# Order of the last stage of an attention and expert block: rotations two groups ahead across sequences, normalisation inside the next sequence

## The chip, the core and the metric

The kernel runs on one core of a Trainium2 chip. The metric is the device time of one execution in microseconds. Its engines are named as in the profile: PE is TensorE (matrix products; PEld its weight loads), DVE is VectorE, ACT is ScalarE, POOL is GpSimd, and SP issues most transfers.

## What is computed

The input x has 8 sequences of 512 tokens with 512 channels. A layer normalisation gives xn; an attention part s and a gate g are computed from it, and the output is x + s * g.

```python
xn = _layernorm(x, axis=-1)
s = _L0_attn_ref(xn, ...)        # linear attention, 16 heads of 32, chunks of 128 tokens
g = _silu(_L0_ffn_ref(xn, ...))  # 16 experts, the best 4 for each token, and a shared one
return x + s * g

# attention, for each sequence
q = _lrpe_rotate(silu(xn @ Wq)); k = _lrpe_rotate(silu(xn @ Wk)); v = xn @ Wv
scores = einsum('bthd,bshd->bhts', qi, ki) * D[None]
o_intra = einsum('bhts,bshd->bthd', scores, vi)
o_inter = einsum('bthd,bhde->bthe', qi * decay_q, S)
S_new = lam_C * S + einsum('bshd,bshe->bhde', ki * decay_k, vi)
x = o * sigmoid(xn @ Wg1 @ Wg2)
x = x * rsqrt(mean of squares over each head + EPS)   # the group normalisation
s = (x * weight) @ Wo
```

Everything is in float32.

## The kernel before

The kernel has three parts. The first normalises all sequences, routes their tokens, computes the shared expert and does the attention of sequences 0 and 1. The second runs the routed experts in blocks of 128 tokens. The third, the last stage, does the attention of sequences 2 to 7 and, beside it, gathers the experts' results for each token tile, adds them up and combines them with the attention's output. The change lies in the last stage.

A sequence's 16 heads are worked in four groups of four heads (G = 4, 128 channels each). For group g of sequence b:

- `key` and `query` (through `rotated`) multiply the transposed input xT by Wk or Wq (four matmuls of 128x512 output, L631), apply silu on ACT (L641), and rotate on DVE with a shuffle, a multiplication by cos, one by sin and an addition (L643 to L647). They write kT and qT, two buffers each.
- `by_token` transposes the rotated keys on PE (L663) and scales them on ACT into kd (L668). `scores` multiplies kd by the values for the states (L684), then keys by queries for all four heads (ps, L695); DVE adds up the states (L699), scales the queries (qd, L714) and multiplies each head's scores by the decay mask (sc, L720); ACT copies the states (L704).
- `output` multiplies states by queries and values by scores into po (L731, L742), and DVE multiplies po by the gate that is in `on` (L746).

`value` makes a tile of 128 tokens of values (pv, L587), copied out by ACT (L591). `gate_1` (L601) and `gate_2` (L617, sigmoid L621) make the gate. When all four groups have their outputs, `squares` (ACT L753, PE pr L756, square root on ACT L760), `inverse` (DVE L764) and `normed` (PE pb L773, four DVE multiplications L778) normalise; `project` multiplies a tile by Wo (pw, L785). The last sequence has forms of its own for its own normalisation (`squares_of`, `normed_of`, L884 to L908) and projection (L915).

PSUM has eight banks: four with tag "a" (the four ps of a group; also pr, pb and the gate), one "k" (transposes and states), one "m" (keys, and the even value tiles), two "d" (queries, odd value tiles, po, pw). Banks of a tag are used in turn, in the order in which the code asks for them, and a bank is free when its last reader is done.

The code of PE is written in its order by hand: `on_pe` ties each group of matmuls behind the one before. The other engines' queues are ordered by the framework's scheduler, except where `behind` ties an instruction to its engine's last one. Each engine works through its queue in order.

`step` in the last stage is `advance`. Each call carries the mixtures of a few token tiles a piece further: four gathers and two additions on POOL (L1215, L1221, L1224), two operations on DVE (m, L1226 and L1230), a silu on ACT (L1233). A new tile starts after every 2.2 calls. `finish` takes a projection's result: `last` multiplies it into the mixture on DVE (L1253; this is pw's reader) and adds x on POOL (L1257).

In `sequence` with `defer` set (sequences 2 to 6) the groups 0 and 1 hold keys and queries of groups 2 and 3 and two projections each of the sequence before; the groups 2 and 3 hold value tiles of the next sequence. After group 3, at the border, come the gate and the last value tile of the next sequence, `squares` and `inverse` of this one, then key, query of group 0, `normed`, key and query of group 1 of the next. `last_sequence` does sequence 7 and three of its groups project sequence 6.

Of the kernel before, what the change touches and what calls it, by code (L numbers as in the profile page):

```python
# [10 lines left out]
F32 = mybir.dt.float32  # L11
# [8 lines left out]
P = 128  # L20
# [3 lines left out]
C = 128  # L24
# [71 lines left out]
def tile_block(ctx: ExitStack, tc: tile.TileContext, a: dict, out: bass.AP):  # L96
# [553 lines left out]
    def key(b, g, ps=None):  # L650
        kT_of[g] = rotated(b, g, "k", wk, ps)

    def query(b, g):
        qT_of[g] = rotated(b, g, "q", wq)
# [94 lines left out]
    def squares(b):  # L749
        pr = bank("a", f"pr_{b}")  # L750
        for g in range(G):
            sq = scr[0].tile([P, N], F32, tag="sc", name=f"sq_{b}_{g}", bufs=4)
            nc.scalar.activation(sq, on_of[b][:, g, :], AF.Square)  # L753
            with on_pe():
                for c in range(NC):
                    nc.tensor.matmul(  # L756
                        pr[c * Q : (c + 1) * Q, :C], lhsT=sel[:, H - HG - g * HG :][:, :Q],
                        rhs=sq[:, c * C : (c + 1) * C], start=(g == 0), stop=(g == G - 1))
        rs = att.tile([P, C], F32, tag="tmp", name=f"rs_{b}", bufs=TMP)
        nc.scalar.activation(rs, pr[:, :C], AF.Sqrt, bias=eps_rms, scale=1.0)  # L760
        rs_of[b] = rs

    def inverse(b):
        nc.vector.reciprocal(rs_of[b], rs_of[b])  # L764
# [16 lines left out]
    def project(b, t):  # L781
        pw = bank("d", f"pw_{b}_{t}")
        with on_pe():
            for g in range(G):
                nc.tensor.matmul(  # L785
                    pw, lhsT=on_of[b][:, g, t * P : (t + 1) * P], rhs=wo[:, g, :],
                    start=(g == 0), stop=(g == G - 1))
        return pw
# [10 lines left out]
        query(b, 1)  # L799
        step()  # L800

    def sequence(b, step, projected, before=None, defer=False, also=lambda: None):


        n = b + 1

        def project_tiles(q, ts):
            if q is not None:
                for t in ts:
                    projected(q, t, project(q, t))  # L810


        fill = ([0], [1], [2], [3], [], [], [], [])
        for g in range(G):
            scores(b, g)
            step()
            if g + 2 < G:
                key(b, g + 2)
            else:
                value(n, 2 * (g - 2))  # L820
            if g + 1 < G:
                by_token(b, g + 1)
            project_tiles(before, fill[2 * g])
            step()
            if g + 2 < G:
                query(b, g + 2)
                if g + 3 == G and n not in xT_of:
                    load_xT(n)
            if g + 2 == G:
                value(n, 1)  # L830
            if g == 0 and b not in on_of:
                gate_2(b)
            project_tiles(before, fill[2 * g + 1])
            if fill[2 * g + 1] == [NC - 1]:
                on_of.pop(before, None)
            output(b, g)
            if defer and g + 2 == G:
                gate_1(n)
            step()
        v_of.pop(b)  # L840
        if n == FIRST:
            gate_1(n)
            squares(b)
            inverse(b)
            value(n, 3)
            normed(b)
            return
        if defer:
            gate_2(n)
        value(n, 3)  # L850
        also()
        squares(b)
        step()
        inverse(b)
        key(n, 0)
        also()
        query(n, 0)
        normed(b)
        also()
        if not defer:  # L860
            step()
        key(n, 1)
        by_token(n, 0)
        if defer:
            step()
        query(n, 1)
        also()
        if not defer:
            gate_1(n)
            project_tiles(b, [0, 1])  # L870
            also()
            project_tiles(b, [2, 3])
            also()
            on_of.pop(b)
        step()

    def last_sequence(b, step, projected, before):

# [43 lines left out]
        for g in range(G):  # L922
            scores(b, g)
            step()
            if g + 2 < G:
                key(b, g + 2)
            if g > 1:
                project_before(2 * g - 3)
            if g:
                squares_of(g - 1)  # L930
            if g + 1 < G:
                by_token(b, g + 1)
            step()
            if g + 2 < G:
                query(b, g + 2)
            if g in (1, 2):
                project_before(2 * g - 2)
                normed_of(g - 1)
            output(b, g)
            step()  # L940
# [357 lines left out]
        nc.gpsimd.memset(blocked[j], 0.0)  # L1298
    other.append(comb)
    enter(FIRST, ps=ahead[0])  # L1300
    for b in range(FIRST, B):
        if b + 1 < B:
            load_xT(b + 1)
            sequence(b, advance, finish, b - 1 if b > FIRST else None, True)
        else:
            last_sequence(b, advance, finish, b - 1)
    while active or late or steps[1] < len(tiles):
        advance()
    right.close()
# [54 lines left out]
```

## Time and profile before

| | us |
|---|---|
| median of 3 runs | 1167.91 (1167.41 to 1173.99) |
| the profiled execution | 1174.44 |
| its span | 1172.6 |
| first query product of the last stage starts | 724.56 |
| first key product of sequence 3, 4, 5, 6, 7 starts | 780.94, 854.93, 930.79, 1009.95, 1090.66 |
| ACT table loads in the last stage | 18 of 1.28 each |

The profile is of one execution. A line of the timeline gives the start, the time to the end of the merged instructions, the engine, the line of the code, the operation, the tiles written and read, and their sizes. Ends of matmuls are modelled, and the next one starts before the one before has ended; so durations of blocks on PE are taken from start to start. The four matmuls of a product are eight in the trace. A line of stretches gives, for each engine, busy time and number of instructions, then the granted clock of PE as a share, the share of the DMA engines and the rate.

### The profile page before, as it was taken

Reading aid. Unit: us, or ns where it says so; the run is one execution under the profiler, and the core shown is the slowest. Engines: PE = TensorE matmul, PEld = TensorE weight load, DVE = VectorE, ACT = ScalarE, POOL = GpSimd, SP = SyncE. Lnnn points to the kernel's source line nnn. Section 1 sums busy time; section 2 is a strip of 40 time slices with the busy share of each in tenths; the row PEclk is TensorE's granted clock in tenths of the full one; section 3 lists DMA queues with packets and bytes.
Section 4 is the critical chain, followed back from the end, with each engine's and each line's share of the span. In section 5 each row is a group of like instructions: output and inputs, shape, how many; then the busy total and the mean of one; then the engine's idle time right before and its main releaser. Section 6 shows DMA issues by size and latency. Waiting matters only on the chain. (4 is left out here: it accounts for less than half of the span.)

```text
span 1172.6 us, 21692 instructions
## 1 busy us (share of the span) xinstructions
PE 1138.4 (97%) x7780; PEld 697.9 (60%) x7780; DVE 713.8 (61%) x1496; ACT 460.9 (39%) x1042; POOL 451.9 (39%) x432
## 2 busy tenths in 40 slices
PE   7999999989999999999999999999999989999997
PEld 4455554456577776777777775555645545546453
DVE  6358726896134443444444445968979597697784
ACT  3224424255264443444444442253251522522541
POOL 3213103200223332333333332763877857858111
PEclk9999999998999999999999999999999999999999
DMA  9976421390769999889999996932747637534012
GB/s 333 316 268 216 157 97 46 111 350 1 230 151 228 231 227 219 226 229 228 220 237 225 234 225 207 337 100 93 259 117 220 189 105 245 147 122 145 19 38 72
DMA packets 163787, 217.45 MB, mean 185 GB/s; under 512 B 89824, under 2 KB 99168, under 8 KB 161760
## 3 DMA queue, kind: packets, MB, share of 16 engines
q1 hardware_dynamic: 142272, 144.14, 40.7%
q0 software_dynamic: 21120, 70.34, 22.1%
q8 instruction: 65, 1.06, 0.4%
q10 hardware_dynamic: 288, 1.57, 0.4%
q14 instruction: 42, 0.34, 0.1%
HBM read 125.73 MB, written 72.43 MB: 169 GB/s over the span
## 5 line engine op out<-in xcount | busy, mean ns | idle before, releaser
L1112 PE MATMUL pgu<-wexp,xt 128*128 x1088 | 257.6, 380 | 1.2 <-ACT xt L1093 0.7
L1112 PEld LDWEIGHTS pgu<-wexp,xt 128*128 128x128 f32 x1088 | 206.4, 190 | 87.5 <-issue 30.5
L1071 POOL DMA_INDIRECT xg<-xn_d,slot x79 | 74.9, 949 | 240.6 <-DVE y L1142 157.6
L1095 ACT COPY xt<-pl 128x512 uint16<-128x512 uint16 x136 | 104.3, 767 | 139.4 <-DMA pl<-xg 80.0
L1117 DVE TENSOR_TENSOR slb<-slb,pgu 128x128 f32<-128x128 f32 x136 | 39.1, 288 | 192.8 <-ACT slb L1116 192.8
L1215 POOL DMA_INDIRECT yg<-y_d,place x128 | 142.7, 1115 | 30.0 <-issue 18.2
L1133 PE MATMUL py<-wexp,hT 128*128 x272 | 139.3, 594 | 0.0
L587 PE MATMUL pv<-wv,xT 128*128 128x512 f32 x256 | 122.2, 614 | 3.8 <-DMA xT<-xT_d 2.7
L631 PE MATMUL pk<-xT,wk 128*128 128x512 f32 x256 | 118.3, 603 | 0.0
L631 PE MATMUL pq<-xT,wq 128*128 128x512 f32 x256 | 115.9, 593 | 0.3 <-PEq L1177 0.3
L785 PE MATMUL pw<-wo,on 128*128 128x512 f32 x224 | 105.7, 621 | 6.7 <-DVE m L1253 6.2
L1257 POOL TENSOR_TENSOR xo<-xo,m 128x512 f32<-128x512 f32 x31 | 45.6, 1471 | 136.3 <-DVE m L1253 128.2
L1071 POOL DMA_INDIRECT more<-xn_d,slot x57 | 53.8, 945 | 109.3 <-DVE y L1142 108.4
L720 DVE TENSOR_TENSOR sc<-ps,dmask 128x512 f32<-128x512 f32 x128 | 79.1, 677 | 1.0 <-PE ps L695 0.9
L631 PEld LDWEIGHTS pq<-xT,wq 128*128 128x128 f32 x256 | 47.3, 191 | 52.7 <-issue 51.7
L785 PEld LDWEIGHTS pw<-wo,on 128*128 128x128 f32 x224 | 43.0, 198 | 59.2 <-issue 48.7
L1142 DVE TENSOR_SCALAR y<-py,xg 128x512 f32<-128x512 f32 x79 | 59.3, 751 | 29.5 <-PE py L1133 29.3
L587 PEld LDWEIGHTS pv<-wv,xT 128*128 128x128 f32 x256 | 46.7, 195 | 50.2 <-issue 42.7
L631 PEld LDWEIGHTS pk<-xT,wk 128*128 128x128 f32 x256 | 46.2, 190 | 50.0 <-issue 47.5
L1116 ACT ACTIVATE slb<-pgu 128x128 f32<-128x128 f32 x136 | 37.9, 278 | 79.8 <-PE pgu L1112 79.3
L704 ACT COPY blocked<-state 32x96 f32<-32x96 f32 x96 | 30.7, 320 | 86.5 <-DVE state L699 85.6
L1142 DVE TENSOR_SCALAR y<-py,more 128x512 f32<-128x512 f32 x57 | 42.7, 750 | 19.7 <-PE py L1133 19.5
(173 smaller groups left out, 1738.4 us busy)
## 6 DMA issues: line engine op xcount, KB each, us to landing
y_d<-y SPq DMA_DIRECT2D x136, 256.0 KB, 3.1
wexp<-in_experts SPq DMA_DIRECT2D x14, 768.0 KB, 9.8
sh_d<-sh SPq DMA_DIRECT2D x32, 256.0 KB, 2.9
m<-sh_d SPq DMA_DIRECT2D x32, 256.0 KB, 4.7
xo<-in_x SPq DMA_DIRECT2D x32, 256.0 KB, 3.5
out<-xo SPq DMA_DIRECT2D x31, 256.0 KB, 2.2
x<-in_x SPq DMA_DIRECT2D x7, 1024.0 KB, 7.6
xT_d<-xT SPq DMA_DIRECT2D x7, 1024.0 KB, 8.5
```

What stands on the lines that cost most here:

```text
L587: nc.tensor.matmul(pv, lhsT=xT_of[b][:, k, t * P : (t + 1) * P], rhs=wv[:, k, :], start=(k == 0), stop=(k == KC - 1))
L631: nc.tensor.matmul(ps, lhsT=w[:, k, g * P : (g + 1) * P], rhs=xT_of[b][:, k, :], start=(k == 0), stop=(k == KC - 1))
L720: nc.vector.tensor_tensor(s, pss[j].rearrange("p (c t) -> p c t", t=C), dmask[:, g * HG + j].unsqueeze(1).to_broadcast([P, NC, C]), ALU.mult)
L785: nc.tensor.matmul(pw, lhsT=on_of[b][:, g, t * P : (t + 1) * P], rhs=wo[:, g, :], start=(g == 0), stop=(g == G - 1))
L1071: nc.gpsimd.indirect_dma_start(out=row(i), out_offset=None, in_=xn_d, in_offset=bass.IndirectOffsetOnAxis(ap=slot[:, i : i + 1], axis=0))
L1095: nc.scalar.copy(xt[:, KP:, :].bitcast(U16).rearrange("p k (t h) -> p h k t", h=2), turned(i).rearrange("p (h k) t -> p h k t", h=2))
L1112: nc.tensor.matmul(pg[:, : 2 * F], lhsT=xt[:, k, :], rhs=wflat[:, bass.ds(off + k * 2 * F, 2 * F)], start=(k == 0), stop=(k == KC - 1))
L1117: nc.vector.tensor_tensor(sl, sl, pg[:, F : 2 * F], ALU.mult)
L1133: nc.tensor.matmul(py, lhsT=hT_of.pop(i), rhs=wflat[:, bass.ds(off_of.pop(i) + KC * 2 * F, D)], start=True, stop=True)
L1142: gone.append(nc.vector.tensor_scalar(y, py, row(i).bitcast(F32)[:, bass.ds(at, 1)], None, ALU.mult).ins)
L1215: nc.gpsimd.indirect_dma_start(out=yg, out_offset=None, in_=y_d, in_offset=bass.IndirectOffsetOnAxis(ap=place[:, r, g : g + 1], axis=0))
L1257: nc.gpsimd.tensor_tensor(xo, xo, m, ALU.add)
```

## The change

Sequences 2 to 6 get a function of their own, `rolling`; `sequence` keeps only what sequences 0 and 1 use. In `rolling` each group has the key and the query that are two groups ahead, across the border into the next sequence; one value tile of the next sequence; and, from sequence 3 on, projections of the sequence before: one in group 1 ahead of the value tile and one after the query, one in group 2 and one in group 3. The first gate product is behind group 2's output, the second in group 3. `squares`, `inverse` and `normed` of the sequence before move from the border into group 0, also in `last_sequence`. The squares get their own tag with two buffers in the last stage, where they had four of the scores' tag, and rs gets its own buffer. The load of xT is issued after the query of group 1, one sequence further ahead, and once before the loop.

```diff
--- before.py
+++ after.py
@@ -749,14 +749,17 @@
     def squares(b):
         pr = bank("a", f"pr_{b}")
         for g in range(G):
-            sq = scr[0].tile([P, N], F32, tag="sc", name=f"sq_{b}_{g}", bufs=4)
+            sq = scr[0].tile(
+                [P, N], F32, tag="sq" if carry else "sc", name=f"sq_{b}_{g}",
+                bufs=2 if carry else 4)
             nc.scalar.activation(sq, on_of[b][:, g, :], AF.Square)
             with on_pe():
                 for c in range(NC):
                     nc.tensor.matmul(
                         pr[c * Q : (c + 1) * Q, :C], lhsT=sel[:, H - HG - g * HG :][:, :Q],
                         rhs=sq[:, c * C : (c + 1) * C], start=(g == 0), stop=(g == G - 1))
-        rs = att.tile([P, C], F32, tag="tmp", name=f"rs_{b}", bufs=TMP)
+        rs = scr[0].tile([P, C], F32, tag="rs", name=f"rs_{b}") if carry else att.tile(
+            [P, C], F32, tag="tmp", name=f"rs_{b}", bufs=TMP)
         nc.scalar.activation(rs, pr[:, :C], AF.Sqrt, bias=eps_rms, scale=1.0)
         rs_of[b] = rs
 
@@ -799,18 +802,10 @@
         query(b, 1)
         step()
 
-    def sequence(b, step, projected, before=None, defer=False, also=lambda: None):
+    def sequence(b, step, projected, also=lambda: None):
 
 
         n = b + 1
-
-        def project_tiles(q, ts):
-            if q is not None:
-                for t in ts:
-                    projected(q, t, project(q, t))
-
-
-        fill = ([0], [1], [2], [3], [], [], [], [])
         for g in range(G):
             scores(b, g)
             step()
@@ -820,7 +815,6 @@
                 value(n, 2 * (g - 2))
             if g + 1 < G:
                 by_token(b, g + 1)
-            project_tiles(before, fill[2 * g])
             step()
             if g + 2 < G:
                 query(b, g + 2)
@@ -828,14 +822,9 @@
                     load_xT(n)
             if g + 2 == G:
                 value(n, 1)
-            if g == 0 and b not in on_of:
+            if g == 0:
                 gate_2(b)
-            project_tiles(before, fill[2 * g + 1])
-            if fill[2 * g + 1] == [NC - 1]:
-                on_of.pop(before, None)
             output(b, g)
-            if defer and g + 2 == G:
-                gate_1(n)
             step()
         v_of.pop(b)
         if n == FIRST:
@@ -845,8 +834,6 @@
             value(n, 3)
             normed(b)
             return
-        if defer:
-            gate_2(n)
         value(n, 3)
         also()
         squares(b)
@@ -857,22 +844,57 @@
         query(n, 0)
         normed(b)
         also()
-        if not defer:
-            step()
+        step()
         key(n, 1)
         by_token(n, 0)
-        if defer:
-            step()
         query(n, 1)
         also()
-        if not defer:
-            gate_1(n)
-            project_tiles(b, [0, 1])
+        gate_1(n)
+        for ts in (range(NC // 2), range(NC // 2, NC)):
+            for t in ts:
+                projected(b, t, project(b, t))
             also()
-            project_tiles(b, [2, 3])
-            also()
-            on_of.pop(b)
+        on_of.pop(b)
         step()
+
+    def rolling(b, step, projected, before):
+
+
+        n = b + 1
+
+        def project_before(t):
+            if before is not None:
+                projected(before, t, project(before, t))
+
+        for g in range(G):
+            scores(b, g)
+            step()
+            ahead = (b, g + 2) if g + 2 < G else (n, g + 2 - G)
+            key(*ahead)
+            if g == 0 and before is not None:
+                squares(before)
+                inverse(before)
+            if g:
+                project_before((0, 2, 3)[g - 1])
+            if g + 1 == G:
+                on_of.pop(before, None)
+                gate_2(n)
+            step()
+            value(n, g)
+            by_token(*((b, g + 1) if g + 1 < G else (n, 0)))
+            query(*ahead)
+            if g == 1 and n + 1 < B:
+                load_xT(n + 1)
+            step()
+            if g == 0 and before is not None:
+                normed(before)
+            if g == 1:
+                project_before(1)
+            output(b, g)
+            if g + 2 == G:
+                gate_1(n)
+            step()
+        v_of.pop(b)
 
     def last_sequence(b, step, projected, before):
 
@@ -928,11 +950,16 @@
                 project_before(2 * g - 3)
             if g:
                 squares_of(g - 1)
+            else:
+                squares(before)
+                inverse(before)
             if g + 1 < G:
                 by_token(b, g + 1)
             step()
             if g + 2 < G:
                 query(b, g + 2)
+            if g == 0:
+                normed(before)
             if g in (1, 2):
                 project_before(2 * g - 2)
                 normed_of(g - 1)
@@ -1298,12 +1325,10 @@
         nc.gpsimd.memset(blocked[j], 0.0)
     other.append(comb)
     enter(FIRST, ps=ahead[0])
+    load_xT(FIRST + 1)
     for b in range(FIRST, B):
-        if b + 1 < B:
-            load_xT(b + 1)
-            sequence(b, advance, finish, b - 1 if b > FIRST else None, True)
-        else:
-            last_sequence(b, advance, finish, b - 1)
+        (rolling if b + 1 < B else last_sequence)(
+            b, advance, finish, b - 1 if b > FIRST else None)
     while active or late or steps[1] < len(tiles):
         advance()
     right.close()
```

## Prediction

> **What bounds the kernel now.** I read the page first, then the busy times of the last stage cut at the first key product of each sequence, then what TensorE waited for, then its instructions in order of time with those of ACT and DVE beside them.
>
> ```profile
> span 1172.6 us, 21692 instructions
> PE 1138.4 (97%) x7780; PEld 697.9 (60%) x7780; DVE 713.8 (61%) x1496; ACT 460.9 (39%) x1042; POOL 451.9 (39%) x432
> ```
>
> TensorE sets the time. What the change can win is the time in which TensorE waits in the last stage, and what it can lose is new waits there. Each stretch below holds one border of sequences and the groups up to the next (us, then busy us and count for each engine, the granted clock, DMA):
>
> ```profile
> 780.94:854.93 73.99, 73.99 (x645) 40.63 (x645) 59.70 (x92) 28.18 (x64) 42.78 (x35) 1.00 0.47 154
> 854.93:930.79 75.86, 74.56 (x645) 40.49 (x645) 63.13 (x93) 29.31 (x66) 58.33 (x50) 1.00 0.60 182
> 930.79:1009.95 79.16, 76.20 (x645) 41.37 (x645) 62.37 (x94) 28.72 (x65) 56.92 (x47) 0.98 0.53 165
> 1009.95:1090.66 80.71, 77.52 (x645) 41.96 (x645) 63.13 (x92) 28.05 (x64) 58.07 (x48) 0.98 0.45 135
> ```
>
> The same 645 matmuls take 73.99, 75.86, 79.16 and 80.71 us. DVE is busy for 60 to 63 us of them, so it has room on average, and is late only in places. TensorE in order of time, two pieces (a bracket gives the idle time before, and what ended it):
>
> ```profile
> 1016.94 1.18 PE L773 MATMUL pb<-rs,wge 16*128 16x128 f32 x32
> 1021.91 3.60 PE L631 MATMUL pq<-xT,wq 128*128 128x512 f32 x8
> 1025.44 0.40 PE L684 MATMUL pk<-v,kd 128*32 128x32 f32 x24
> 1025.84 2.95 PE L695 MATMUL ps<-qT,kT 32*128 32x128 f32 x32
> ```
> ```profile
> 961.81 5.40 PE L785 MATMUL pw<-wo,on 128*128 128x512 f32 x8 [2.96 <-DVE m L1253]
> 967.04 0.83 PE L731 MATMUL po<-qd,blocked 128*128 128x128 f32 x6
> 967.80 1.08 PE L742 MATMUL po<-sc,v 128*32 128x128 f32 x32
> 968.70 0.37 PE L684 MATMUL pk<-v,kd 128*32 128x32 f32 x24
> 969.00 1.17 PE L695 MATMUL ps<-qT,kT 32*128 32x128 f32 x32
> ```
> ```profile
> 1041.53 5.40 PE L785 MATMUL pw<-wo,on 128*128 128x512 f32 x8 [1.91 <-DVE m L1253]
> ```
>
> The two projections run at half the clock after their wait: 5.2 us from start to start where others take 3.43, so 1.8 us each. The scores at 1025.84 take 2.9 us instead of 1.1, because their four PSUM banks are freed by the four multiplications of `normed` (L778), here on DVE, with two lines of ACT:
>
> ```profile
> 1016.21 2.27 DVE L645 TENSOR_TENSOR kT<-sk,cos 128x512 f32<-128x512 f32 x1
> 1021.10 0.73 DVE L643 STREAM_SHUFFLE swq<-sq 128x512 f32<-128x512 f32 x1
> 1025.11 2.47 DVE L778 TENSOR_TENSOR on<-on,pb 128x512 f32<-128x512 f32 x4
> 1028.60 0.67 DVE L645 TENSOR_TENSOR kT<-sk,cos 128x512 f32<-128x512 f32 x1
> ```
> ```profile
> 1013.66 1.28 ACT L641 ACT_TABLE_LOAD   x1 [1.71 <-PE pk L631]
> ```
>
> **What it removes.** The excess over 73.99 is 1.9 + 5.2 + 6.7 = 13.8 us. The waits account for most: four times a projection behind DVE (6.2 us in the list of waits), two half-clock pieces (3.6), the scores (1.8), the group sums at 1088 (1.1). In the new order a group has key, [projection], value, transposes, query, [projection], output. A projection's PSUM bank is wanted again after a value product and transposes (3.8 us) instead of a query product (3.4), and a group has one projection, one group two, where two groups had two each. I credit all 13.8, 0.8 for a pause at 760.6 in sequence 2, and 1.6 because a sequence has 10 instead of 12 runs of wide products (a run's last product costs 3.63 instead of 3.43: 2 x 0.2 x 4 sequences). Sum: 16.2.
>
> **What it adds.** The number of matmuls and DMAs stays. New is where `squares` and `normed` of sequence b-1 stand: in group 0 of sequence b (3 to 7, five times), between the scores of group 0 and of group 1, which use the same four "a" banks. Three waits follow.
>
> *Scores of group 1 behind `normed`.* Let E be the end of group 0's query product. TensorE then has pb 1.10 (1016.94 to 1018.04), output 1.66 and state products 0.30 (967.04 to 969.00), and wants the scores at E + 3.06. Before, a key and a query product stood in between. In the built order DVE has the query rotation ahead of the multiplications: silu starts at E + 0.15 and takes 0.60, the shuffle starts at E + 0.79; shuffle 0.62, cos 0.60, sin 0.72, add 0.69 (start to start, undisturbed), four multiplications 2.47: E + 5.89. That is a wait of 2.8 us at least. POOL is busy for over half of these stretches, and an operation like the one at 1016.21 takes 2.27 instead of 0.67 beside it; by the means of their groups (cos 1.05, add 1.09 against 0.68) this adds 0.8. In sequences 4, 5 and 6 the order has one mixture operation (means 0.90 and 0.98, I take 0.9) ahead as well. In 3, 4 and 7 ACT's table load follows its wait for the query product, as at 1013.66, and adds 1.28. So 2.8 + 0.8 + 1.3 = 4.9, then 5.8, 4.5, 4.5 and, with POOL busy for 10 of the last 81 us, 2.8 + 1.3 = 4.1: 23.8. Without any collision it is 20.0 (a mixture operation then adds 0.65), with both operations hit as at 1016.21 in sequences 3 to 6 it is 33.
>
> *Group sums (`pr`) after group 0's key.* The squares get two buffers instead of four. Two wait for nothing; the third and fourth stand on ACT behind the key's silu: key end + 0.2 + 0.60 + 0.62 + 0.52 + 0.1 and the last part 0.25 make 2.3 us for a block of 1.0, so 1.3. The first part also needs the first score bank read. From the end of the query product before, TensorE is there after 1.66 + 0.30 + 1.10 + 3.54 = 6.6. In 4 and 5 DVE needs 0.79, rotation 2.63, the output's gate 0.60, three mixture operations 2.0, state 0.28, qd 0.47 and the first score 0.68: 7.4, by the means of the groups 1.7 more. That is 0.8 to 2.5 late, and the two squares then follow (0.25 + 0.2 + 0.62 + 0.52 + 0.1 + 0.25 - 1.0 = 0.9): 1.7 to 3.4. In 3 and 6 it has one mixture operation, no qd, but starts behind the output: 6.6, by the means 7.7, so 1.3 to 2.0. I take 2.0 + 3.4 + 3.4 + 2.0 + 1.3 = 12.1; low 7.3, high 15 if DVE is as late in all of 3 to 6.
>
> *Key and value in one bank.* Values 0 and 2 use bank "m", like the key. In sequence 2 nothing stands between: 0.2 + 0.60 + 0.1 of silu, twice, 1.8. Later a projection or the group sums hide it.
>
> *The clock.* Both waits of 1.9 and 3.0 us in the rows were followed by half clock, 1.8 us each; waits of 4 to 6 us should be too, but part of the slow stretch then falls into the wait. I take 1.3 x 5 = 6.5; 3.6 if two of five are hit, 9 if all in full.
>
> The Trainium skill ("TensorE: Matmul & The Clock Gate", "What's actually happening") speaks against a gap too, but has the clock fall after at least one idle window of about 3.4 us. These rows fell after less. By the page only a wait that covers a whole window costs, so perhaps two of the five: the sum would be some 4 us lower; I go by the rows.
>
> **Priced at nothing.** `load_xT` for two sequences on now waits on SP for group 1's query product; it lands in 8.5 us and is wanted some 45 us later; if SP were held up by outputs, its 8.5 us would show at value 0. Five more table loads (23 against 18, 1.28 each) fall on an ACT busy for 28 us of 75; the three on the path are counted. There are 16 instead of 15 `advance` calls a sequence; POOL's queue, with its gathers behind the additions L1257, waited 128 us for DVE and so runs ahead; if it did not, DVE's mixture operations and then the scores would wait, 1 to 3 us a tile. In groups 1 and 3 the query product waits for DVE's reading of the projection; value product and transposes give 3.8 us, and DVE reaches it about 1.8 us earlier; that margin gone, each us costs one.
>
> **Sum.** 23.8 + 12.1 + 1.8 + 6.5 - 16.2 = 28.0 us. The profiled execution took 1174.44 (span 1172.6 and 1.8 around it), so 1202. The median of the runs is 1167.91, 6.5 less, and I put the same difference on it: 1196. All low ends give 20.0 + 7.3 + 1.8 + 3.6 - 16.2 = +16.5, 1184; all high ends, with 13 won, 33 + 15 + 1.8 + 9 - 13 = +46, 1214.
>
> **Rivals.**
> A. *The border waits are hidden and the gain stays.* Break-even is (16.2 - 1.8) / 5 = 2.9 us a border. If DVE took the multiplications as soon as `pb` is there, they would end at E + 1.2 + 2.47, a wait of 0.6; with the squares ready in time and no fall of the clock: 1167.9 - 16.2 + 1.8 + 3 = 1156; with 1.3 a border for the squares 1163. For it: DVE has 11 us to spare in a sequence, and the first stretch shows next to no wait. Against: the built order has the rotation first, and one engine works in order. 12%, half of it over 1% faster.
> B. *The waits are there but shorter.* No collisions, no clock fall beyond one or two, half of the sums' wait: 20 + 3.6 + 1.8 + 2 - 16.2 = +11, 1179. For: an evener load gives DVE slack. Against: the means of the rows. 14%.
> C. *DVE never catches up after a border*: the query product of group 1 waits for L1253, by as much as it has in hand (1.8), and the clock falls twice a border (1.8): 5 x 3.6 = 18 more, 1214. For: 63 us of DVE work. Against: 17 us of TensorE work before group 1's output. 8%.
> D. *The change doesn't do what it says.* The built order has two rotations, one value product and about one projection in every group, so I give it nothing of its own.
>
> The forecast has 66%. About 1% (11.7 us) is what a measurement of this kernel can tell from no change. Faster by more: 0.06. Within: 0.06 of A and most of B, 0.15. Slower by more: 0.79. The range 1172 to 1211 leaves out A and C.
>
> **What would show it.** Right: TensorE's list of waits names L778 (scores) and ACT's squares (`pr`) once a border, the waits on L1253 are gone, sequences 3 to 6 last 80 to 84 us each, the clock falls near the borders. Wrong: stretches of 74 to 76 us, scores of group 1 with 1.2 us everywhere, or DVE multiplying right after `pb`.

## The result and the profile after

The changed kernel takes 1217.07 us (median of 4 runs, 1216.09 to 1217.75) against 1168.75 for the kernel before beside it: a ratio of 1.0389, 95% interval 1.0359 to 1.0419. It is 3.9% slower. The forecast, 1196 with a range of 1172 to 1211, had the direction and the places, but was 21 us too low. The profiled execution took 1217.75.

The head of the page after:

```profile
span 1216.0 us, 21663 instructions
PE 1159.6 (95%) x7780; PEld 710.7 (58%) x7780; DVE 695.6 (57%) x1496; ACT 468.8 (39%) x1047; POOL 447.1 (37%) x432
```

The span grew by 43.4 us and TensorE's busy time by 21.2 with the same 7780 matmuls. DVE has the same 1496 instructions and was busy for less, so nothing was added to it; it is needed at a worse moment. The last stage cut at the scores of group 0 of each sequence, so that each of these four stretches holds one sequence (3 to 6) with the normalisation of the one before (us, then busy us of each engine, granted clock, DMA):

```profile
800.28:883.60 83.32, 78.45 (x654) 43.48 (x644) 55.33 (x95) 30.20 (x65) 49.71 (x42) 0.96 0.47 149
883.60:969.01 85.41, 78.93 (x654) 44.00 (x644) 60.83 (x96) 30.21 (x65) 59.63 (x51) 0.96 0.54 169
969.01:1055.69 86.68, 80.55 (x655) 43.63 (x644) 63.48 (x95) 30.78 (x66) 58.91 (x50) 0.96 0.51 164
1055.69:1139.64 83.95, 79.22 (x654) 42.83 (x644) 52.12 (x90) 30.03 (x64) 36.22 (x31) 0.96 0.26 78
```

All four take 83 to 87 us (the prediction named 80 to 84), where the four of before took 74 to 81, and the granted clock is 0.96 in each instead of 0.98 to 1.00. What TensorE waited for in the last stage (total us, times, longest):

```profile
PE ps L695 <- DVE on L781: 14.8, 8, 3.0
PE pr L758 <- ACT sq L755: 5.2, 5, 1.5
PE pr L758 <- DVE sc L720: 3.8, 2, 2.5
PE pv L587 <- ACT sk L641: 3.8, 2, 3.0
```

The list names the waits that the prediction named: scores behind the multiplications of `normed` (now L781), the group sums behind ACT's squares and behind the first score bank, a value behind its key's silu. The projections' waits for their reader (6.2 us before) are gone. One border in order of time, sequence 4, rows of PE, ACT and DVE (a bracket gives the idle time before, and what ended it):

```profile
899.10 1.17 PE L776 MATMUL pb<-rs,wge 16*128 16x128 f32 x32
899.25 1.28 ACT L641 ACT_TABLE_LOAD   x1 [2.28 <-PE pq L631]
...
901.83 2.26 DVE L645 TENSOR_TENSOR qT<-sq,cos 128x512 f32<-128x512 f32 x1
...
904.61 0.67 DVE L781 TENSOR_TENSOR on<-on,pb 128x512 f32<-128x512 f32 x1
905.21 1.58 DVE L647 TENSOR_TENSOR qT<-qT,swq 128x512 f32<-128x512 f32 x1
905.34 1.15 PE L695 MATMUL ps<-qT,kT 32*128 32x128 f32 x8 [3.00 <-DVE on L781]
906.71 0.74 DVE L1253 SCALAR_TENSOR_TENSOR m<-m,sg,yg 128x512 f32<-128x512 f32 x1
907.38 1.87 DVE L781 TENSOR_TENSOR on<-on,pb 128x512 f32<-128x512 f32 x3
908.10 3.27 PE L695 MATMUL ps<-qT,kT 32*128 32x128 f32 x24 [1.61 <-DVE on L781]
```

The product `pb` is done at 900.2, but its readers on DVE start at 904.61 and 907.38: the table load, the silu and the rotation come first, one rotation step takes 2.26 instead of 0.68, and a mixture operation stands among the multiplications. TensorE stops twice, for 3.00 and 1.61 us. Then the clock falls. Stretches of half clock (us, TensorE's busy time, granted clock), three of the eight:

```profile
906.90:913.70 6.80, 5.60 (x27) 0.50 0.29 81
978.60:982.00 3.40, 3.40 (x12) 0.50 0.48 117
995.70:999.10 3.40, 3.40 (x12) 0.50 0.26 77
```

With the other five it is 41 us at half clock in the last stage; before there were 6.8. Every sequence from 2 to 7 has one or two.

### The profile page after: what moved, and what is told of

The parts are those of the page before. It is cut to its first block, busy times and chain, and to the rows that moved or that the text cites. A ratio compares the mean times of both kernels' runs of the same rounds, so it can differ in the third digit from the quotient of the medians.

```text
span 1216.0 us, 21663 instructions
## 1 busy us (share of the span) xinstructions
PE 1159.6 (95%) x7780; PEld 710.7 (58%) x7780; DVE 695.6 (57%) x1496; ACT 468.8 (39%) x1047; POOL 447.1 (37%) x432
## 5 line engine op out<-in xcount | busy, mean ns | idle before, releaser
L1242 POOL DMA_INDIRECT yg<-y_d,place x128 | 137.1, 1071 | 32.0 <-issue 19.1
L587 PE MATMUL pv<-wv,xT 128*128 128x512 f32 x256 | 125.1, 626 | 7.9 <-ACT sk L641 3.8
L631 PE MATMUL pk<-xT,wk 128*128 128x512 f32 x256 | 124.9, 631 | 0.0
L788 PE MATMUL pw<-wo,on 128*128 128x512 f32 x224 | 100.1, 594 | 0.6 <-DVE on L781 0.6
L631 PEld LDWEIGHTS pk<-xT,wk 128*128 128x128 f32 x256 | 48.9, 201 | 54.1 <-issue 51.6
L695 PE MATMUL ps<-qT,kT 32*128 32x128 f32 x1024 | 53.2, 302 | 16.3 <-DVE on L781 14.8
L591 ACT COPY v<-pv 128x512 f32<-128x512 f32 x32 | 18.7, 585 | 103.1 <-PE pv L587 103.1
```

The lines of the kernel that those rows point to most:

```text
L587: nc.tensor.matmul(pv, lhsT=xT_of[b][:, k, t * P : (t + 1) * P], rhs=wv[:, k, :], start=(k == 0), stop=(k == KC - 1))
L631: nc.tensor.matmul(ps, lhsT=w[:, k, g * P : (g + 1) * P], rhs=xT_of[b][:, k, :], start=(k == 0), stop=(k == KC - 1))
L695: nc.tensor.matmul(pss[j][:, cs], lhsT=kT[hs, cs], rhs=qT[hs, cs], start=True, stop=True)
L788: nc.tensor.matmul(pw, lhsT=on_of[b][:, g, t * P : (t + 1) * P], rhs=wo[:, g, :], start=(g == 0), stop=(g == G - 1))
L1242: nc.gpsimd.indirect_dma_start(out=yg, out_offset=None, in_=y_d, in_offset=bass.IndirectOffsetOnAxis(ap=place[:, r, g : g + 1], axis=0))
```

## The experiments

The experiments start from two versions, `t_before` and `t_after`, in which the expert blocks, ahead of the last stage, transpose their rows on TensorE instead of half of them by DMA. The order on DVE, ACT and POOL in the last stage is that of `before` and `after`, instruction by instruction, and PE has the same matmuls. The kernels ran in five groups, each on another chip; beside them the kernel before had medians of 1183.3, 1181.8, 1172.3, 1171.1 and 1183.1, so across groups the ratio to it is what can be compared.

| kernel | group | median us | ratio to before, interval |
|---|---|---|---|
| t_before | 1 | 1205.49 | 1.0201 (1.0161 to 1.0241) |
| t_after | 1 | 1251.57 | 1.0594 (1.0538 to 1.0650) |
| e1b_norm_before_query | 1 | 1228.68 | 1.0397 (1.0353 to 1.0441) |
| e3b_fill_wait | 1 | 1243.82 | 1.0536 (1.0490 to 1.0581) |
| e2b_four_squares | 2 | 1238.68 | 1.0479 (1.0438 to 1.0520) |
| e4b_value_bank | 2 | 1247.46 | 1.0552 (1.0506 to 1.0598) |
| e6_no_norm_after | 2 | 1207.49 | 1.0216 (1.0176 to 1.0257) |
| e7_no_norm_before | 2 | 1189.29 | 1.0058 (1.0034 to 1.0082) |
| e5_norm_alone | 3 | 1233.30 | 1.0525 (1.0460 to 1.0590) |
| e8_no_norm_bank | 3 | 1196.63 | 1.0226 (1.0157 to 1.0296) |
| v4_all | 3 | 1211.41 | 1.0354 (1.0286 to 1.0421) |
| v3_late_norm | 3 | 1213.13 | 1.0355 (1.0292 to 1.0418) |
| t_before_2 | 4 | 1196.76 | 1.0209 (1.0180 to 1.0238) |
| e7_again | 4 | 1183.33 | 1.0099 (1.0074 to 1.0124) |
| e9_no_norm_rolled | 4 | 1195.31 | 1.0208 (1.0186 to 1.0229) |
| v6_early_sums | 4 | 1212.14 | 1.0354 (1.0331 to 1.0376) |
| e10_no_norm_bank_m | 5 | 1190.56 | 1.0062 (1.0036 to 1.0089) |
| v7_early_sums | 5 | 1224.52 | 1.0346 (1.0303 to 1.0390) |

**The base.**

> The kernel before with one thing changed outside the last stage, so that further kernels can be built on it: in the expert blocks TensorE transposes all four quarters of a block's rows (two transposes of 0.11 us more for each of 136 blocks), where a transfer turned two of them; the rows are stored in plain float32 for it. The queues of the last stage are the same instruction by instruction. Theory: 30 us more than the kernel before, about 1198, and the last stage lasts as long as before, 441 to 447 us from its first query product.

> The changed kernel with the same edit in the expert blocks. Theory: 30 us more than the changed kernel, about 1247, and 45 to 49 us more than the kernel before with this edit; all of that difference lies in the last stage, and the waits at the border are the same five times three. Rival: part of the loss comes from how the expert blocks hand over to the last stage; then the difference is another than 45 to 49.

```diff
-            for k in range(KP):
+            for k in range(KC):
                 nc.tensor.transpose(
```

The pair differs by 46.1 us, as the originals do (48.3), and the trace of t_after has the same waits as `after`, 12.3 us at the scores instead of 14.8. t_before itself took 22 us more than the kernel before where 30 was expected, and its last stage 452.1 us where 441 to 447 was.

**Theory 1, the place of the normalisation.** What costs is that in group 0 TensorE asks for `pr` and for the score banks before DVE and ACT can have answered, and that half clock follows such pauses. The first rival: keys and queries that run ahead of the border make DVE late by themselves.

*The multiplications ahead of group 0's query.*

> The changed kernel (with the edit in the expert blocks) with `normed` ahead of group 0's query product instead of behind it, in rolling and in the last sequence. Theory 1 (the scores of group 1 wait for the four multiplications of `normed`, which stand on DVE behind the rotation of a query whose product has only just ended, and the clock falls after the wait): the multiplications now run under the query product; the wait at the scores (28 us over five borders above the usual 1.1) and the half-clock keys behind it (7 us) go, a wait of about 1 us a border for the reciprocal comes at pb. 25 to 32 us less than that base. Theory 2 (DVE is simply behind after a border, whatever stands in front): the wait moves to the states or the transposes of group 1; 0 to 10 us less.

```diff
             by_token(*((b, g + 1) if g + 1 < G else (n, 0)))
+            if g == 0 and before is not None:
+                normed(before)
             query(*ahead)
...
-            if g == 0 and before is not None:
-                normed(before)
```

It took 22.9 us off, half of the loss and a little less than expected. The scores no longer wait for `normed`. In TensorE's list of waits a new one stands in their place:

```profile
PE pb L774 <- DVE rs L765: 2.7, 2, 1.9
```

The sums wait as before (9.0 us), and `pb`, now earlier, waits for the inverse. Half clock in the last stage falls from 44.4 to 13.7 us. So the 28 us at the scores are real and come from the order on DVE; 2.7 of them come back at `pb`.

*The pause filled.*

> The changed kernel (with the edit in the expert blocks) with one more product of four matmuls, 3.43 us, whose result nobody reads, ahead of group 1's scores at the five borders: 17 us of matmuls more. Theory 1 (TensorE idles there for more than 3.4 us, and the idling costs the clock): the product fits into the wait, the clock does not fall behind it, and the kernel is faster than its base by 5 to 12 us. Rival a (the slow matmuls behind the border have another cause): no change or up to 5 us slower. Rival b (there is no true wait at the scores, TensorE is the bound): 17 us slower.

```diff
+    def fill(b):
+        ps = bank("m", f"fill_{b}")
+        with on_pe():
+            for k in range(KC):
+                nc.tensor.matmul(ps, lhsT=wq[:, k, :P], rhs=xT_of[b][:, k, :], ...)
...
+            if g == 0 and before is not None:
+                fill(b)
             output(b, g)
```

Five useless products of 3.43 us, 17 us in all, did not make the kernel slower: by the medians it is 7.8 us faster, though the two sets of four executions just overlap (1237.89 to 1248.23 against 1246.55 to 1256.26). The last stage of t_after and then of this kernel:

```profile
748.00:1247.50 499.50, 463.77 (x3760) 252.10 (x3760) 331.66 (x552) 170.99 (x373) 263.72 (x225) 0.95 0.42 134
```
```profile
748.90:1236.10 487.20, 462.03 (x3800) 246.25 (x3800) 333.48 (x552) 171.42 (x373) 265.11 (x225) 0.99 0.43 137
```

With 40 more matmuls TensorE is busy for 1.7 us less: half clock falls from 44.4 to 10.2 us and the mean grant rises from 0.95 to 0.99. The 17.2 us of products were paid for by 18.9 us of slow running that went; of the waits for `normed`, 12.3 us, 1.6 are left. So a pause lowers the clock, and here the slow running that went cost more than the 10.7 us of pauses that went with it. e1b shows the same without any product more.

*Four buffers for the squares, and the values of the first rolled sequence in another bank.*

> t_after with four buffers for the squares instead of two (and 13 instead of 14 for the gathered rows, to have the room). In t_after (1251.6 us) the group sums waited 5.2 us for ACT's third and fourth square, which stand on ACT behind the silu of the key, and 3.5 for the first score bank. Theory 1 (each wait of the normalisation at a border is paid in full): the 5.2 us go and a part of the half clock behind them, so 1243 to 1247. Rival (the scores of group 1 stand behind the same rotation and multiplications on DVE, so TensorE comes there earlier and waits longer): 0 to 2 us less, 1249 to 1252, with the wait for the normalised output grown from 12.3 to 15 to 17 us.

```diff
-                bufs=2 if carry else 4)
+                bufs=4)
```

> t_after with the values 0 and 2 of the first rolled sequence in PSUM bank d in place of bank m, which the key before them uses. In the trace of the changed kernel the two values waited 3.8 us there for the silu of the key, and half clock followed them. Theory 1: wait and slow stretch both go, 5 to 7 us less than t_after (1251.6), so 1245 to 1247. Rival (the key and query rotations of that sequence are bound on DVE, and the wait moves to the next product): 0 to 3 us less, 1249 to 1252.

```diff
-            value(n, g)
+            value(n, g, "d" if before is None else None)
```

The squares gave 12.9 us, more than either case had: the 5.2 of waits went, half clock fell to 30.7 us, and the scores did not give it back (their waits 12.3 before, 11.4 after). The bank gave 4.1, between the two cases, but the intervals of the two ratios overlap, so how much it gave is not shown. The waits of the value are gone from its list, and no other entry grew in their place.

*The normalisation alone.*

> t_before with one part of the change alone: the group sums, the inverse and the multiplications of a sequence are moved into group 0 of the next one, and its projections follow in groups 0 (last), 1 and 3; keys, queries and values stay where the kernel before has them. Theory 1 (the place of the normalisation is the loss, whatever the keys do): the scores' excess of 20 to 28 us, the sums' 8 to 12 and 8 to 15 of half clock, less 4 us of waits for the projections' reader: t_before (1205.5) + 30 to 45, 1236 to 1250. Rival (it takes both parts together; in the old order the group 0 has less on DVE): 1206 to 1222.

```diff
+            if g == 0 and before is not None:
+                squares(before)
+                inverse(before)
...
+            if g == 0 and before is not None:
+                normed(before)
```

Its ratio of 1.0525 against 1.0201 and 1.0209 for t_before is 3.2%, about 37 us, of the 46 that the whole change costs (1245 on group 1's scale, where 1236 to 1250 was expected). Its edit includes the two buffers for the squares. The first two of its waits carry the same names:

```profile
PE ps L693 <- DVE on L779: 7.2, 6, 2.2
PE pr L756 <- DVE sc L718: 5.3, 2, 3.3
```

So moving the normalisation into group 0, with the two buffers, is enough for most of the loss; the rival, that it needs the rolled keys, falls.

**What is the rolled order worth without it?** Five kernels leave out the group sums, inverse and multiplications of sequences 2 to 6.

> t_after without the group sums, the inverse and the multiplications of sequences 2 to 6 (their share of the computation is left out; the projections then take the output as it is). It shows what rolling the keys and queries gives by itself. Theory 1 (the loss is the normalisation in group 0, with the clock behind it): the products left out are 2.1 us a sequence, 10.5 in all; the scores' and the sums' waits (28 and 12 us of excess in the changed kernel) and some 12 of half clock go with them: 1251.6 - 62 = 1185 to 1193, at most 2 us more than the same edit made in the kernel before. Rival (the keys and queries that run two groups ahead load DVE and ACT unevenly whatever stands in group 0): the products and half of the waits, 1215 to 1232.

> t_before without the group sums, the inverse and the multiplications of sequences 2 to 6, as in e6_no_norm_after. Theory 1: in the old order the normalisation is nearly covered, so little but its 10.5 us of products goes, and the scores' excess of 1 to 2 us a border: 1205.5 - 10.5 - 4 = 1187 to 1194. Under the prediction's account the rolled order then wins by the 16 us it was credited with, so e6 would be near 1175; if the credit was too large by what one slow execution of the kernel before lent it, e6 and e7 lie within 8 us of each other. Rival (the old order, too, pays for the normalisation): 20 us or more less than t_before.

```diff
             if g == 0 and before is not None:
-                squares(before)
-                inverse(before)
+                rs_of[before] = None
...
-            if g == 0 and before is not None:
-                normed(before)
```

Taking it out of t_after won 44.1 us, out of t_before 16.2. But e6 stands 18.2 above e7, where theory 1 had 2. Its list of waits names the cause:

```profile
PE pv L585 <- ACT sk L639: 9.8, 6, 2.6
```

Key and value 0 share bank "m"; without `pr` in between, the value waits for the key's silu at every border, not in sequence 2 alone.

> e6_no_norm_after (1207.5 us) with all values of the rolled sequences in PSUM bank d. Without the group sums in between, e6 had a value product right behind a key product in the same bank, six times, 9.8 us of waits for the silu of the key, and half clock behind them; it stood 18 us above e7_no_norm_before (1189.3). Theory 1 (this pair alone makes the 18): 9.8 us and some 3 to 7 of slow products go, 1190 to 1195, so that rolling by itself neither wins nor loses. If the credit of 16 us in the prediction was right, 1175 to 1180. Rival (the rolled order itself is late on DVE): 1200 to 1206, with a wait for a DVE tile in place of the silu.

```diff
-        pv = bank("d" if t % 2 else "m", f"pv_{b}_{t}")
+        pv = bank("d" if carry or t % 2 else "m", f"pv_{b}_{t}")
```

> e7_no_norm_before once more, for the next kernel: 14 to 18 us less than t_before_2, as in the run before (1189.3 against 1205.5).

It came out 13.4 us below t_before_2.

> The rolled order without the group sums, the inverse and the multiplications of sequences 2 to 6, with values in bank d only where no projection stands between a key and its value (group 0, and all of the first rolled sequence). It is the rolled order with neither the wait for the silu of the key (e6) nor that for the reader of the projection, 9.2 us, which appeared when all values were in bank d (e8). It measures what the prediction credited with 16.2 us. If the credit was right: 13 to 16 us less than e7_again. If the waits for the projections in the kernel before are only some 5 to 8 us in a usual execution (4.6 in t_before): 4 to 8 less. If the rolled order has nothing to give: within 3 us of e7_again.

```diff
-            value(n, g)
+            value(n, g, "d" if g == 0 or before is None else None)
```

e8 and e9 are misses: 1.0226 and 1.0208, no better than the 1.0216 of e6. The silu wait is gone and a new one is there, in e9:

```profile
PE pq L629 <- DVE m L1253: 9.1, 4, 3.6
```
```profile
914.30 3.60 PE L786 MATMUL pw<-wo,on 128*128 128x512 f32 x8
917.73 3.60 PE L585 MATMUL pv<-wv,xT 128*128 128x512 f32 x8
921.16 0.49 PE L661 MATMUL pk<-ident,kT 128*128 128x128 f32 x3
...
925.22 1.12 PE L629 MATMUL pq<-xT,wq 128*128 128x512 f32 x2 [3.57 <-DVE m L1253]
```

Projection, value 3 and query take turns in the two banks "d", so the query waits until DVE has read the projection. It is the wait for which the prediction gave DVE 1.8 us in hand; here DVE is up to 3.6 late. (This profiled execution, 1187.30, was e9's fastest; the others took 1195 to 1201.)

> e9_no_norm_rolled with the values of groups 1 to 3 in bank m, where a projection stands between a key and its value. In e9 (1195.3 us, e7_again 1183.3) the query product of group 3 waited four times, 9.1 us, for DVE's reading of the projection ahead of the value, because projection, value and query take turns in the two banks d. With the values in m the query takes the bank of the output before. If this wait is all that holds the rolled order back: 9 to 12 us less than e9, 1183 to 1187, level with e7_again. If DVE is late in those groups in general: 0 to 4 less, and the wait is at the next product that DVE or ACT feeds.

```diff
-            value(n, g, "d" if g == 0 or before is None else None)
+            value(n, g, "d" if g == 0 or before is None else "m")
```

With the values of groups 1 to 3 in "m" no wait for another engine above 0.4 us is left, and the ratio is 1.0062, level with the old order's 1.0058 and 1.0099. (In the profiled executions the last stage took 437.1 us in e9 and 436.3 in e10, which has 4.4 us of pauses that no engine accounts for; the gain shows in the medians.) So rolling keys and queries ahead, with its own bank conflicts removed, wins nothing that these intervals can tell from zero (0.4% at most by the ratios), and as written it loses over 1% even without the normalisation.

**Can the normalisation be covered in the rolled order?**

> t_after with three of the edits together: the multiplications ahead of group 0's query (22.9 us less by itself), four buffers for the squares (12.9 less), all values in bank d (4.1 less). If they are separate waits: 1251.6 - 40 = 1212. If one wait gives way to the next (the pb product was already 2.7 us behind the inverse in the first of them, and comes earlier once the squares are early): 1220 to 1228. Under 1205.5 (t_before) it comes only if the half clock goes altogether.

> t_after with the normalisation spread out: all four squares on ACT right behind the key of group 0, the group sums on TensorE behind the value product, the multiplications in group 1 behind its value product and ahead of its query, projections 0, 1, 2, 3 in groups 1, 2, 2, 3; values in bank d, four buffers for the squares. Theory 1 (what costs is only that TensorE asks for a result before 3 to 7 us of other products have covered it): the scores of group 1 find their banks free, the sums wait for nothing: excess near that of e7, 1197 to 1207, that is t_before (1205.5) or a little less. Rival (DVE has 63 us of work in 75 and any place for 2.5 us more delays the next rotation): 1212 to 1225.

The first has the edits of e1b and e2b and `value(n, g, "d")`; the second:

```diff
-            value(n, g)
+            value(n, g, "d")
+            if g == 0 and before is not None:
+                squares(before)
+                inverse(before)
+            if g == 1 and before is not None:
+                normed(before)
```

> t_before once more, so that the three kernels beside it are compared on one chip: within 1% of its 1205.5 us, and 1.5 to 2.5% above the kernel before.

> The rolled order with the normalisation cut at other places: the squares of groups 0 to 2 on ACT at the end of their own sequence and the fourth ahead of the next key's silu; the group sums behind group 0's key, in bank d, so that they wait neither for ACT nor for the first score bank; the multiplications behind group 0's value product, which covers the root and the inverse, and ahead of the query product, which covers them; the first sequence's values in bank d. Theory 1 (only the cover counts): no wait over 1 us at a border, half clock at most in two stretches, 5 to 12 us less than t_before_2. Rival (the 10 us of multiplications and squares at the border make DVE late for the rotations wherever they stand): 3 to 12 us more, as v4_all (1211.4).

```diff
-        pr = bank("a", f"pr_{b}")
+        pr = bank("d" if carry else "a", f"pr_{b}")
...
             value(n, g, "d" if before is None else None)
+            if g == 0 and before is not None:
+                normed(before)
+            if g + 1 == G:
+                for q in range(G - 1):
+                    squared(b, q)
```

> v6_early_sums (1212.1 us) with three waits of its trace taken away: the inverse ahead of the rotation of group 0's key on DVE (pb behind it 6.5 us in 4), value 0 in bank d (silu of the key 3.2 us in 4), the values of groups 1 to 3 in bank m (query product behind the projection's reader 1.9 us). If they are separate: 10 to 14 us less with the half clock, 1198 to 1202, level with t_before_2 (1196.8). If DVE is late at the border wherever things stand: 1206 to 1212.

```diff
         nc.scalar.activation(s, ps, AF.Silu)
+        first()
         w_ = att.tile(...)
```

In the second, `squares` issues only the matmuls; ACT's squares stand behind the key. In v7 `first` issues the sums and the inverse. t_before_2 came out as expected, 15 us below v6. All four stand at 1.035, 2.3% below t_after and 1.4% above t_before: none beats the old order. Scaled by the kernel before to group 1, where the numbers expected come from, v4 and v3 are at 1225, the second case of each: in v4 one wait gave way to the next, and in v3 the waits stand at other products than a rotation's, the projection behind the multiplications (3.9 us), the scores behind the gate (3.3) and `pb` behind the root (2.1). v6 missed both of its cases; v7, scaled to group 4, is at 1212, the end of its second. In v4 and v6 `pb` waits for the inverse, 9.9 and 6.5 us, in v7 11.7. v7 was to bring the inverse forward, but the built order on DVE kept it behind the key's rotation:

```profile
831.76 0.37 ACT L769 ACTIVATE rs<-pr,eps_rms 128x128 f32<-128x128 f32 x1
...
833.60 0.69 DVE L646 TENSOR_TENSOR kT<-kT,swk 128x512 f32<-128x512 f32 x1
834.21 0.95 DVE L773 RECIPROCAL rs<-rs 128x128 f32<-128x128 f32 x1
```

The root is there at 832.13, the inverse starts at 834.21. So v7 did not try what it was meant to, and whether an inverse ahead of the rotation would bring the rolled order under the old one stays open.

## Why the prediction was right about the mechanism and wrong about the size

Excess is the time of a block of matmuls from start to start beyond what such blocks usually take (a product 3.43, scores 1.10, sums 1.01, states 0.30). The stage from the first query product to the end took 492.3 us, before 448.1: 44.2 longer. The forecast of 28.0 for it was 16.2 too low.

| step of the prediction | predicted | measured |
|---|---|---|
| scores of group 1 behind `normed` | 23.8 (4.9, 5.8, 4.5, 4.5, 4.1) | 28.1 (6.2, 7.9, 4.1, 5.1, 4.8) |
| group sums behind group 0's key | 12.1 (2.0, 3.4, 3.4, 2.0, 1.3) | 12.0 (2.0, 2.4, 4.2, 2.1, 1.3) |
| key and value in one bank, sequence 2 | 1.8 | 4.3 |
| clock, outside of these waits | 6.5 | 13.6 |
| removed waits and the rest | -16.2 | -13.8 (44.2 less the others) |
| sum | 28.0 | 44.2 |
| from the profiled execution to the median | -6.5 | -0.7 |

**The clock** is the step that failed most: "I take 1.3 x 5 = 6.5", and even its high end was 9. The key products behind the scores lost 1.3 to 1.8 each (7.2 in five), about what was predicted; but the value products lost 6.4 more, 3.0 at 771 behind the wait in sequence 2, 1.6 at 979 and 1.8 at 1064 behind the group sums:

```profile
771.26 6.64 PE L587 MATMUL pv<-wv,xT 128*128 128x512 f32 x8 [3.02 <-ACT sk L641]
...
978.94 5.21 PE L587 MATMUL pv<-wv,xT 128*128 128x512 f32 x8
...
1063.54 5.40 PE L587 MATMUL pv<-wv,xT 128*128 128x512 f32 x8
```

The prediction counted one fall a border. There are two kinds of pause at a border, `pr` and `ps`, 11 to 18 us apart, and in sequences 5 and 6 each was followed by a fall of its own. Two falls a border were rival C's price, but its cause, the query behind L1253, is not in the list of waits. In sequences 3, 4 and 7 only the pause at the scores was followed by one, of twice the length. What `pr` costs in clock varies: with its waits kept (9.0 and 8.5 us) and those at the scores gone, e1b and e3b ran 13.7 and 10.2 us at half clock. The Trainium skill ("TensorE: Matmul & The Clock Gate", "What's actually happening") puts the fall after at least one idle window of 3413 ns; no wait in the list is longer than 3.0 us, yet there were eight slow stretches, so the rows decide against reading it as a safe bound on a pause.

**The scores** were mis-sized by 4.3, 3.4 of it in sequences 3 and 4. The chain was as described, table load included, but in sequence 4 the mixture operation stood between the multiplications and not ahead of them, and two steps were hit, 2.26 and 1.58 instead of 0.68: near the case that made the high end. TensorE's list books 14.8 of the 28.1 us as waits; in the rest lies half clock that begins inside the scores (906.9 in sequence 4), so the clock cost more than its own row says.

**Key and value in sequence 2** were priced by TensorE and the silu alone, 0.9 each. The first cost 1.0, the second 3.3: the silu stood on ACT behind the copies of the states, and those behind a DVE that was late after a rotation step of 2.43 us. ACT's queue ahead of the silu was not counted.

**The gain** of 13.8 is what the other rows leave, 2.4 under the 16.2 credited. Part of the credit was misread: 1.6 rests on 3.63 us for the last product of a run, where the prediction's own row has 3.53 (1021.91 to 1025.44). And the gain was booked as if it were independent of the loss. e9 speaks against that: with the border's waits gone, the query waits 9.1 us for DVE; in `after` and, but for 1.2 us, in e6, which pause at the border, that wait is not in the list. Rival A's 1156 was out of reach by these runs: with the whole normalisation left out and the bank conflicts removed, the rolled order (e10) was level with the old one. The old order won 16.2 us by leaving it out, of which 10.5 are products that the changed kernel keeps, so some 6 us is an estimate of what hiding it could win, not 12.

**The median.** "I put the same difference on it" was a step without evidence. Before's profiled execution was 6.5 us above its median, after's 0.7. Some 5.8 of the 21 us are due to this and 16.2 to the sum; the stages ahead of the last one took 0.9 less. Why that execution was slower can't be told without a second trace of the original kernel.

One reading priced at nothing was off as well: 8.5 us is the median of the store xT_d<-xT, while the five loads of xT in that stage landed in 4.9 to 8.7 us, 6.5 in the middle. No term rests on it.

## What to carry to other kernels

A reduction and its broadcast-back (sums, root, inverse, multiply) need cover on TensorE at two places, and a queue in order adds whatever stands ahead of it on ACT and DVE to the latency: count that queue from the last operand to the last reader, and put products of that length in between. A short pause of a busy TensorE is to be priced with the half clock that may follow it, at every pause; a filler product can be cheaper than idling. And a wait that vanishes at one bank may show up at the next: a gain and a loss in the same stretch are not independent terms of a sum.

## What the runs showed of the hardware that was not expected

The stretches of half clock begin on a grid: 770.4, 821.6, 906.9, 978.6 and 995.7 lie 51.2, 85.3, 71.7 and 17.1 us apart, which is 15, 25, 21 and 5 times 3.413, and in `after` they last one or two such steps. The Trainium skill ("TensorE: Matmul & The Clock Gate", "What's actually happening") states a free-running window of 3413 ns, which these numbers agree with. In the step ahead of each of the eight stretches TensorE was idle for 1.2 to 2.8 us of the 3.4, never for all of it; six other steps with 1.2 to 1.7 us of idle time were followed by no fall. So a pause cost none, one or two steps, and its length alone does not tell which; whether its place on the grid does was not tried.

In groups 1, 2 and 5, where the kernel before took 1182 to 1183 us, runs of small matmuls show pauses, mostly of up to 0.5 us, that no engine accounts for (2.6 us in 7 at the states in t_after; up to 1.1 each in v7). In groups 3 and 4, with the kernel before at 1171 to 1172, they are absent from the lists. As each group had a chip of its own, they may belong to the chip; their cause was not tried.
